# Three changes in a two-layer graph kernel: when layer 1's transfers go out, how many denominators are taken together, and which ready piece TensorE takes

## The chip, the cores and the metric

The kernel runs on one core of a Trainium2 chip. The core has TensorE (PE in the profile; matrix products, with PEld loading the weights), VectorE (DVE), ScalarE (ACT), GpSimd (POOL) and SyncE (SP), which here mostly issues the transfers. The metric is the time of one execution on the device in microseconds (us), lower being better.

## The reference, cut to what matters

Two layers of a graph network on 3327 nodes with 256 features. Layer 0 does two steps; in each, the features are multiplied by the row-normalised adjacency matrix (Xf) and by an attention matrix of which only the largest entries, 90% of each row's mass, are kept (Xa). Layer 1 is a graph attention with four heads of 64 features.

```python
h = relu(layernorm(x))
R = (adj + eye) / rowsum(adj + eye)
for n in range(2):                               # layer 0
    A  = top_p(softmax(q(Xa) @ k(Xa).T), 0.9)    # rows summed to 1 again
    Xf = R @ Xf
    Xa = A @ Xa
    Z  = Z + Xf @ U1[n].T + Xa @ U2[n].T
x = x + layernorm(h + Z)

hp = (relu(layernorm(x)) @ W).reshape(n, 4, 64)  # layer 1
e  = leaky_relu(s[:, :, None] + d[:, None, :])   # s, d: two numbers per node and head
e  = where(adj > 0, e, -inf)
x  = x + elu(softmax(e, axis=2) @ hp)
```

## The kernel before, in words

The nodes lie in 26 tiles of 128 (padded to 3328). All matrix products are in float32, so that the profile shows two TensorE records for one product.

**The planner.** The code doesn't issue instructions one after the other. It puts *pieces* of work into a `Plan` (L481, `put`), each with an engine, a length in us as its author estimates it, a rank (the due time, as it were: lower is earlier), the pieces that it needs, the buffers that it takes and gives back, and a lag until others see its result. `order` (L507) walks through an imagined time and, whenever an engine is free, takes among the pieces that are ready and whose buffers are free the one of lowest rank (L553). The pieces are then issued in the order that comes out, and each engine and each queue works through its own instructions strictly in that order, whatever the real times are.

**Layer 0.** For each of the two steps n and each row tile i there are two chains:

- *Attention* of row i. `search` (L1502): TensorE makes the logits, ScalarE their exponentials (tile e, or qq for every fifth row); ScalarE counts over the row for two or three guesses of the threshold with GpSimd's arithmetic between, then VectorE takes a window of candidates, sorts them, chooses the threshold and drops what lies below. `attention` (L1559): VectorE transposes 32 x 32 blocks, the three parts of the row go to DRAM (`put_blocks`, L1121) and come back turned (`get_blocks`, L1126, four transfers for each part), and TensorE multiplies them with the features in pieces of four, the last of six (`attend_blocks`, L1133, into the PSUM bank acca). All rows go by memory except the last row, 25, of the second step, which TensorE turns itself (L1090, L1108). Row 24 is thus the last turned row that travels through memory.
- *The adjacency row* t (`full`, L1594): SyncE loads 128 x 512 pieces of the transposed adjacency matrix (L1152) into six rotating tiles named at, and TensorE multiplies them in pieces of two (`some`, L1158) into the PSUM bank accf. There is one such bank. At the end of a row it is copied out by ScalarE or VectorE (L1169, L1172, L1175, L1179) before the next row can begin. In the second step GpSimd then adds a base that SyncE fetched (L1183, L1192).

After the second step each row is normalised (`finish2`, L1402) and projected with layer 1's weights (L1440, L1449); ScalarE's L1435 is the normalisation's last step before the transposes of L1440.

**Layer 1** (`attend_neighbours`, L1619). The result's columns are done in four blocks b of 832. Within a block, the loop j runs over the 26 tiles of source nodes. SyncE loads adjacency pieces (L1734; for j = 0 and 1 of the first block L1721, into the tile kt), ScalarE makes a mask of them (L1743 and L1744; L1728 and L1729), VectorE builds a tile of masked scores for the four heads (L1755, four instructions) from one of seven rotating tiles and from numbers broadcast over the partitions (`broadcast`, L1681, transfers L1688 into qq, for odd blocks into c). TensorE multiplies it with the features (products, L1771, into pl) and with the weights of the softmax's denominators (sums, L1785, into acca and accf). A tile of scores is given back when its sums are done. The sums of JG = 2 tiles are put together behind the products of those two; the last six j of the last block go one by one, in halves. When a block is done, ScalarE copies the banks out (L1843 to L1857), TensorE transposes (L1882), and the elu and the sum with x follow.

The transfers that open layer 1 have their own conditions: the first two adjacency pieces and the broadcast of block 0 need `open_heads` (all logits done, the counts of all rows done, the rows in qq done), the later adjacency pieces need all logits done.

Of the kernel before, what the change touches and what calls it, by code (L numbers as in the profile page):

```python
# [21 lines left out]
NT = 26  # L22
# [449 lines left out]
class Plan:  # L472
# [34 lines left out]
    def order(self):  # L507
# [17 lines left out]
        while len(out) < len(self.pieces):  # L525
            while events and events[0][0] <= clock:
                _, _, p, what = heapq.heappop(events)
                if what == "end":

                    held = sum(max(0.0, min(z, clock) - max(a, p["at"])) for a, z in holds[-12:])  # L530
                    end = p["at"] + p["length"] + held
                    if end > clock + 1e-6:
                        now[p["engine"]] = end
                        heapq.heappush(events, (end, p["k"], p, "end"))
                    else:
                        finish(p, clock)
                    continue
                if what not in ("", "own"):
                    free[what] += 1
                    continue  # L540
                for q in p["then"]:
                    if (q["engine"] == p["engine"]) == (what == "own"):
                        q["left"] -= 1
                        if not q["left"]:
                            for e in q["on"]:
                                ready[e].append(q)
            for e, queue in ready.items():
                if now[e] > clock or not queue:
                    continue
                can = [p for p in queue if all(free[b] >= p["take"].count(b) for b in p["take"])]  # L550
                if not can:
                    continue
                p = min(can, key=lambda q: q["rank"])  # L553
                for k in p["on"]:
                    ready[k].remove(p)
                p["engine"] = e
                p["length"], p["fn"], p["lag"], p["hold"] = p["on"][e]
                for b in p["take"]:
                    free[b] -= 1
                p["at"] = clock  # L560
                now[e] = clock + p["length"]
                if p["hold"]:
                    holds.append((clock, clock + p["hold"]))
                if e == "POOL":
                    heapq.heappush(events, (now[e], p["k"], p, "end"))
                else:
                    finish(p, now[e])
                out.append(p)
            if events and events[0][0] <= clock:
                continue  # L570
            times = [t for e, t in now.items() if t > clock and ready[e]] + ([events[0][0]] if events else [])
            later = [t for t in times if t > clock]
            if not later:
                if len(out) < len(self.pieces):
                    raise RuntimeError("the plan stands still")
                break
            clock = min(later)
# [10 lines left out]
def fast(  # L588
# [58 lines left out]
    with ExitStack() as l0:  # L647
# [911 lines left out]
        def attention(row, rank, total, drops, right):  # L1559
# [17 lines left out]
            for g in range(3):  # L1577
                b = plan.put(
                    "DVE", 1.17 if g < 2 else 1.44, rank - 1.001, row.turn_blocks, g, needs=[drops[g]]
                )  # L1580
                b = plan.put("SP", 0.5, rank - 1.0, row.put_blocks, g, needs=[b], lag=7.0)
                b = plan.put("", 0.0, -90.0, lambda: None, needs=[b], lag=0.0)
                come.append(
                    [plan.put("SP", 0.6, rank - 1.0, row.get_blocks, g, o, needs=[b], lag=5.0) for o in range(4)]
                )
            for j in range(0, NT - 2, 4):
                js = range(j, j + 4 if j < 20 else NT)
                a = plan.put(
                    "PE", 0.432 * len(js), rank, row.attend_blocks, js, needs=[come[j // 8], a, right],
                    take=["acca"] * (j == 0), give=[own_e[row.n][row.i]] * (j == 20),  # L1590
                )
            return plan.put("ACT", 0.4, rank - 2.7, row.attended, needs=[a, total], take=["xa"], give=["acca", "sc"])

        def full(n, t, rank, right, after):  # L1594
# [7 lines left out]
            for j in range(0, NT, 2):  # L1602
# [2 lines left out]
                    "PE", 0.437 * 2, rank, f.some, range(j, j + 2), needs=[a, loads[j // JC], right[j : j + 2], own if t in (j, j + 1) else None],  # L1605
                    take=["accf"] * (j == 0), give=["at"] * last,
                )
            if n == 1:
                a = plan.either(
                    ("ACT", 0.4, f.scaled_by_s), ("DVE", 0.45, f.scaled_by_v), -90.0, needs=[a], give=["accf"]  # L1610
# [8 lines left out]
        def attend_neighbours(rows, ends, done, fulls):  # L1619
# [1 line left out]

            W = NP // 4
            C = W // 2
            JG = 2
            LATE = 6
            logits_done = [r.pieces["logits"] for r in rows]
            freed = [p for p in done]
# [6 lines left out]
            def open_heads():  # L1634
                both = wpool.tile([P, NT, P], F32, name="qq").rearrange("p t d -> p (t d)")
                extra["both"] = [both.rearrange("p (h w) -> p h w", h=H)]

                extra["at"] = wpool.tile([P, 2 * W], F32, name="kt").rearrange("p (k w) -> p k w", k=2)
                extra["m"] = scr.tile([P, NP // 2], BF16, name="junk").rearrange("p (k w) -> p k w", k=2)

# [6 lines left out]
                extra["e"] += halves_of("rhs", None)  # L1647

            counted = [r.pieces["counted"] for r in rows]
            fifth = [d for d, name in zip(done, own_e[1]) if name == "e5"]  # L1650
            opened = [plan.put("", 0.0, 59.0, open_heads, needs=[logits_done, counted, fifth], lag=0.0)]
            opened.append(plan.put("", 0.0, 59.0, open_heads2, needs=[fulls, opened], lag=0.0))
            more = plan.put("", 0.0, 59.0, open_more, needs=[freed, opened], lag=0.0)

# [23 lines left out]
            cuts = (0, 7, 13, 20, NT)  # L1678
            spread = [spread_heads(*cuts[k : k + 2]) for k in range(4)]

            def broadcast(b, rank):  # L1681

                lo, hi = b * W, (b + 1) * W
                got, after = [], [spread[: b + 1], opened[b % 2], used_heads[b % 2]]
                for a in range(2):
# [4 lines left out]
                            highs[2 * a : 2 * a + 2, lo:hi].partition_broadcast(P),  # L1690
                        )

                    got.append(plan.put("SP", 0.1, rank, fetch, needs=[after], lag=7.0 + 5.0 * a))
                return got

            last, f_ = {}, None
            used_heads = [None, None]
            evacuated = [None, None]
            both = broadcast(0, 59.5)
            for b in range(4):  # L1700
                lo = b * W
                r0 = 60.0 + 10.0 * b
# [12 lines left out]
                for j in range(NT):  # L1715
# [77 lines left out]

                    own = ["mask"]
                    if b == 0 and j < 2:
                        loads = plan.put("SP", 0.2, rank, load_first, needs=[opened[0]], lag=4.0)
                        m_ = last_m = plan.put("ACT", 1.8, rank, mask_first, needs=[loads, last_m], take=own)
                    else:
                        loads = [
                            plan.put("SP", 0.4, rank, load, g, needs=[logits_done], take=["at"], lag=4.0)  # L1800
                            for g in range(2)
                        ]
                        m_ = last_m = plan.put("ACT", 2.2, rank, mask, needs=[loads, last_m], take=own, give=["at", "at"])
# [20 lines left out]
                        "PE", 1.42, max(rank, r0), product, 1, needs=[x_, y_, evacuated[1]], take=["pl"] * (j == 0)  # L1824
                    )
                    group.append((sums, mine))
                    if len(group) == JG or j == NT - 1 or (b == 3 and j == NT - LATE - 1):
                        for n_, (fn, name) in enumerate(group):
                            last_den = plan.put(
                                "PE", 1.52 - 0.06 * (n_ == 0), max(rank, r0), fn, needs=[last_acc, last_den, done if b == 0 else None],  # L1830
                                take=["acca", "accf"] * (j < JG and n_ == 0), give=[name],
                            )
                        group = []
                used_heads[b % 2] = last_e
# [298 lines left out]
```

## Time and profile before

| | us |
|---|---|
| median of 3 runs | 2049.98 |
| lowest and highest | 2047.79, 2050.27 |
| the profiled execution | 2050.93 |
| its span, first to last instruction | 2049.1 |
| TensorE busy | 2017.5 (98%) |
| VectorE busy | 1688.8 (82%) |
| ScalarE busy | 1298.0 (63%) |
| GpSimd busy | 1025.8 (50%) |
| DMA queue 1, share of 16 engines | 61.9% |

In time, the first 50 us prepare, layer 0's two steps run until about 1570 us, and layer 1 from there to the end. The profile names an instruction by its line in the kernel, its engine, and its output and inputs by the program's names. A wait is idle time of an engine just before an instruction, with the instruction that ended it; the chain is followed back from the last instruction to whatever released each step. The granted clock is TensorE's clock as a share of full speed.

### The profile page before, as it was taken

The numbers are of one execution on the slowest core, as the hardware profiler recorded it, in microseconds if no ns is written. First come the engines' busy times: TensorE is split into PE (matmuls) and PEld (weight loads), VectorE is DVE, ScalarE is ACT, GpSimd is POOL, SyncE is SP. The second block draws the span as 40 slices with busy tenths as digits, with TensorE's granted clock in tenths as the row PEclk, the third lists the DMA queues.
The fourth block names the chain that finished last, engine by engine and source line by source line (L and its number), as shares of the span: only waits on it lengthen the run. The fifth ranks groups of instructions, "written<-read, shape, count | busy, mean of one in ns | idle before, by whom it ended". The sixth has DMA issues, their size and how long they took to land. (4 is left out here: it accounts for less than half of the span.)

```text
span 2049.1 us, 33972 instructions
## 1 busy us (share of the span) xinstructions
PE 2017.5 (98%) x10526; PEld 1398.1 (68%) x10526; DVE 1688.8 (82%) x3763; ACT 1298.0 (63%) x2637; POOL 1025.8 (50%) x2222
## 2 busy tenths in 40 slices
PE   9999999999999999999999999999999999999997
PEld 6577778878777887788887877777876333333332
DVE  5589998987878845888788888888877999999894
ACT  5777777665667417866777777777634456475642
POOL 5377766765566615776777877778752000000001
PEclk9999999999999999999999999999999999999999
DMA  3276777867766776787577677676783354443440
GB/s 96 78 212 180 213 202 195 219 193 208 193 191 189 224 186 198 199 229 215 155 202 210 188 186 207 195 204 188 205 256 119 113 155 133 142 129 115 127 118 26
DMA packets 628991, 358.20 MB, mean 175 GB/s; under 512 B 366810, under 2 KB 581760, under 8 KB 628800
## 3 DMA queue, kind: packets, MB, share of 16 engines
q1 hardware_dynamic: 627904, 355.72, 61.9%
q8 instruction: 86, 1.41, 0.3%
q14 instruction: 105, 0.86, 0.1%
q10 hardware_dynamic: 896, 0.21, 0.0%
HBM read 252.69 MB, written 102.88 MB: 174 GB/s over the span
## 5 line engine op out<-in xcount | busy, mean ns | idle before, releaser
L1133 PE MATMUL acca<-rhs,e 128*128 128x256 f32 x2132 | 474.0, 381 | 4.4 <-DMA e<-blocks 4.4
L964 ACT ACTIVATE junk<-e,sc 128x3327 fp8e5<-128x3327 f32 x147 | 450.8, 3067 | 43.3 <-POOL sc L1001 41.8
L1133 PEld LDWEIGHTS acca<-rhs,e 128*128 128x128 f32 x2132 | 418.7, 197 | 52.3 <-DMA e<-blocks 4.8
L1158 PE MATMUL accf<-main,at 128*128 128x257 f32 x1352 | 316.6, 383 | 4.4 <-ACT f L1169 3.3
L1158 PE MATMUL accf<-c,at 128*128 128x256 f32 x1352 | 310.0, 382 | 6.4 <-DVE main L1175 4.2
L1158 PEld LDWEIGHTS accf<-main,at 128*128 128x128 f32 x1352 | 250.2, 190 | 63.2 <-issue 17.2
L1158 PEld LDWEIGHTS accf<-c,at 128*128 128x128 f32 x1352 | 252.1, 190 | 55.6 <-issue 9.9
L1027 DVE MAX8 cands<-y 128x8 f32<-128x205 f32 (+1 forms) x832 | 242.1, 361 | 3.6
L1744 ACT ACTIVATE junk<-at 128x448 bf16<-128x448 f32 (+1 forms) x204 | 112.2, 550 | 178.3 <-DVE e L1755 111.7
L1934 POOL TENSOR_TENSOR qq<-qq 128x256 f32<-128x256 f32 x4 | 2.9, 730 | 430.8 <-ACT qq L1930 430.7
L1022 DVE SCALAR_TENSOR_TENSOR y<-e,sc 128x1639 f32<-128x1639 f32 x84 | 165.7, 1972 | 48.4 <-POOL sc L1012 47.2
L1771 PE MATMUL pl<-e,main 128*64 128x416 f32 x1024 | 191.9, 517 | 0.0
L909 PE MATMUL pl<-kt,qg 64*128 64x512 f32 (+1 forms) x832 | 173.7, 536 | 1.4 <-ACT qq L926 0.8
L1078 DVE SCALAR_TENSOR_TENSOR e<-e,thr 128x1024 f32<-128x1024 f32 (+1 forms) x126 | 171.2, 1360 | 1.0
L1117 DVE STREAM_TRANSPOSE e<-e 128x1024 f32<-128x1024 f32 (+1 forms) x123 | 164.6, 1338 | 6.2
L926 ACT ACTIVATE e<-pl 128x1024 f32<-128x1024 f32 x123 | 134.9, 1105 | 53.0 <-PE pl L909 49.5
L1771 PEld LDWEIGHTS pl<-e,main 128*64 128x64 f32 x1024 | 69.5, 137 | 109.4 <-issue 91.8
L1755 DVE SCALAR_TENSOR_TENSOR e<-qq,low,junk 128x832 f32<-128x832 f32 x128 | 130.4, 1086 | 7.7 <-DMA qq<-highs 4.0
L1755 DVE SCALAR_TENSOR_TENSOR e<-c,low,junk 128x832 f32<-128x832 f32 x128 | 129.2, 1070 | 4.5 <-issue 3.2
L909 PEld LDWEIGHTS pl<-kt,qg 64*128 64x128 f32 x832 | 71.5, 186 | 85.9 <-issue 71.3
L964 ACT ACTIVATE junk<-qq,sc 128x3327 fp8e5<-128x3327 f32 x35 | 107.4, 3068 | 19.5 <-POOL sc L1001 19.2
L1133 PE MATMUL acca<-rhs,qq 128*128 128x256 f32 x520 | 114.7, 380 | 0.0
(553 smaller groups left out, 3366.6 us busy)
## 6 DMA issues: line engine op xcount, KB each, us to landing
at<-in_adjt_dram SPq DMA_DIRECT2D x414, 256.0 KB
blocks<-e SPq DMA_DIRECT2D x82, 512.0 KB
e<-blocks SPq DMA_DIRECT2D x328, 128.0 KB
blocks<-e SPq DMA_DIRECT2D x41, 640.0 KB
e<-blocks SPq DMA_DIRECT2D x164, 160.0 KB
at<-in_adjt_dram SPq DMA_DIRECT2D x102, 192.0 KB
blocks<-qq SPq DMA_DIRECT2D x20, 512.0 KB
qq<-blocks SPq DMA_DIRECT2D x80, 128.0 KB
```

Source lines behind the costliest of these rows:

```text
L909: T.matmul(pl[:, lo : lo + m], qg[self.n, self.i // 4][half, self.i % 4, :], kt[half, 512 * k : 512 * k + m], start=True, stop=True,)
L926: S.activation(to, pl.rearrange("p (g t q) -> p g t q", g=4, t=2), AF.Exp, accum_out=sums[k])
L964: S.activation(junk[:, :N], self.e[:, :N], fn, bias=t, scale=-1.0, accum_out=dst, saturate=False)
L1022: V.scalar_tensor_tensor(self.y[:, : hi - lo], self.e[:, lo:hi], self.up, self.e[:, lo:hi], ALU.is_lt, ALU.mult, accum_out=(self.h0, self. ...
L1027: V.max(self.cands[:, a * PIECES // 2 + k, :], self.y[:, at[k] - lo : at[k + 1] - lo])
L1078: V.scalar_tensor_tensor(piece, piece, self.thr[:, at : at + 1], piece, ALU.is_gt, ALU.mult)
L1117: V.transpose(part, part)
L1133: T.matmul(self.acc, lhs, rhs[self.n][:, j, :], start=(j == 0), stop=(j == NT - 1))
L1158: T.matmul(self.acc[:, : self.w], self.at[j // JC][:, j % JC, :], self.src[:, j, : self.w], start=(j == 0), stop=(j == NT - 1),)
L1744: S.activation(to, src, AF.Sign)
L1755: V.scalar_tensor_tensor(held["e"][:, k, :], extra["both"][b % 2][:, k, :], low[:, j, k : k + 1], held["mask"], ALU.max, ALU.mult,)
L1771: T.matmul(q["acc"][a][k * FH : (k + 1) * FH, c, :C], main[:, j, h * FH : (h + 1) * FH], held["e"][:, h, c * C : (c + 1) * C], start=(j == 0),
```

## The change

- *The pick of the planner.* Attention's pieces on TensorE by way of memory are marked `spare`, the later pieces of an adjacency row `fill` (j from 16 on, or from 20 on in the second step's rows from 14 on). If the ready piece of lowest rank is spare, and no spare piece waits only for it, then a fill piece is taken in its place if one is ready.
- *Layer 1's transfers.* `open_heads` is split: the broadcast tile needs only the rows that used it (rank 52), the tiles for the first adjacency pieces (`open_first`) still need logits and counts. The first half of block 0's broadcast is put behind the last read of row 23's blocks, the second half and all adjacency loads of layer 1 behind the last read of row 24's.
- *Denominators.* The sums are taken for four tiles at a time: in blocks 1 to 3, and in block 0 from j = 16 on (before that for two). The lengths given to the planner follow.

```diff
                 p = min(can, key=lambda q: q["rank"])
+                if p.get("spare") and not any(q.get("spare") and q["left"] == 1 for q in p["then"]):
+                    p = min((q for q in can if q.get("fill")), key=lambda q: q["rank"], default=p)
...
+            row.pieces["come"] = come
...
                     take=["acca"] * (j == 0), give=[own_e[row.n][row.i]] * (j == 20),
                 )
+                a["spare"] = True
...
                     take=["accf"] * (j == 0), give=["at"] * last,
                 )
+                a["fill"] = j >= (16 if n == 0 or t < 14 else 20)
...
-            JG = 2
...
+            def open_first():
                 extra["at"] = wpool.tile([P, 2 * W], F32, name="kt").rearrange("p (k w) -> p k w", k=2)
                 extra["m"] = scr.tile([P, NP // 2], BF16, name="junk").rearrange("p (k w) -> p k w", k=2)
...
+            turns = [r.pieces["come"][-1][-1] for r in rows if r.i < BLOCKED[1]]
+            came = turns[-1]
             fifth = [d for d, name in zip(done, own_e[1]) if name == "e5"]
-            opened = [plan.put("", 0.0, 59.0, open_heads, needs=[logits_done, counted, fifth], lag=0.0)]
+            opened = [plan.put("", 0.0, 52.0, open_heads, needs=[fifth], lag=0.0)]
+            room = plan.put("", 0.0, 59.0, open_first, needs=[logits_done, counted], lag=0.0)
...
-            def broadcast(b, rank):
+            def broadcast(b, rank, behind=()):
...
-                    got.append(plan.put("SP", 0.1, rank, fetch, needs=[after], lag=7.0 + 5.0 * a))
+                    got.append(plan.put("SP", 0.1, rank, fetch, needs=[after, behind[a : a + 1]], lag=7.0 + 5.0 * a))
...
-            both = broadcast(0, 59.5)
+            both = broadcast(0, 52.0, turns[-2:])
...
-                        loads = plan.put("SP", 0.2, rank, load_first, needs=[opened[0]], lag=4.0)
+                        loads = plan.put("SP", 0.2, rank, load_first, needs=[room, came], lag=4.0)
...
-                            plan.put("SP", 0.4, rank, load, g, needs=[logits_done], take=["at"], lag=4.0)
+                            plan.put("SP", 0.4, rank, load, g, needs=[logits_done, came], take=["at"], lag=4.0)
...
-                    if len(group) == JG or j == NT - 1 or (b == 3 and j == NT - LATE - 1):
+                    if len(group) == (4 if b or j > 15 else 2) or j == NT - 1 or (b == 3 and j == NT - LATE - 1):
                         for n_, (fn, name) in enumerate(group):
                             last_den = plan.put(
-                                "PE", 1.52 - 0.06 * (n_ == 0), max(rank, r0), fn, needs=[last_acc, last_den, done if b == 0 else None],
-                                take=["acca", "accf"] * (j < JG and n_ == 0), give=[name],
+                                "PE", 1.46 + 0.1 * (n_ == 0) + 0.1 * (n_ == len(group) - 1), max(rank, r0), fn, needs=[last_acc, last_den, done if b == 0 else None],
+                                take=["acca", "accf"] * (last_den is None), give=[name],
                             )
```

## The prediction

> **What bounds the kernel now.** First the page's busy times, then the chain of what ended last, then waits, then stretches of time around the place where the attention stage hands over to layer 1. The busy times (engine, busy us, share of the span, instructions):
>
> ```profile
> PE 2017.5 (98%) x10526; PEld 1398.1 (68%) x10526; DVE 1688.8 (82%) x3763; ACT 1298.0 (63%) x2637; POOL 1025.8 (50%) x2222
> ```
>
> TensorE (PE) is busy for all but 31.6 of 2049.1 us, and 15 of those lie in the first 51 and the last 50 us. So an edit gains by fewer TensorE microseconds, by idle gaps in between, or by the clock. The waits of TensorE, longest first (who waited, for whom: us, times, longest):
>
> ```profile
> PE acca L1133 <- DMA e<-blocks: 4.4, 4, 3.4
> PE accf L1158 <- DVE main L1175: 4.2, 8, 0.6
> PE accf L1158 <- ACT f L1169: 3.3, 6, 0.9
> ...
> PE accf L1158 <- ACT main L1172: 1.7, 3, 0.6
> PE accf L1158 <- DVE f L1179: 1.0, 2, 0.5
> ```
>
> Attention (L1133) waits once for long, 3.4 us; the adjacency rows (L1158) wait 20 times (with one for POOL, 0.5 us), 10.7 us, some 0.54 each: the single bank accf is being copied out while the next row wants it. The long wait, in TensorE's order of time (start, length, records, idle before):
>
> ```profile
> 1522.48 1.99 PE L1158 MATMUL accf<-c,at 128*128 128x256 f32 x8 [0.56 <-ACT main L1172]
> 1527.91 11.80 PE L1133 MATMUL acca<-rhs,e 128*128 128x256 f32 x40 [3.43 <-DMA e<-blocks]
> ```
>
> The same 40 records took 8.80 us for the row before. The windows say why (us, busy of each engine, granted clock, DMA share, GB/s):
>
> ```profile
> 1520.00:1530.00 10.00, 5.47 (x19) 3.88 (x18) 8.20 (x23) 0.47 (x1) 3.74 (x4) 0.85 1.02 290
> 1530.00:1540.00 10.00, 10.00 (x40) 8.60 (x40) 7.37 (x28) 0.63 (x2) 5.77 (x14) 0.81 0.67 184
> ```
>
> The granted clock fell to 0.85 and 0.81, so this stall costs 3.43 + (11.80 - 8.80) = 6.4 us. The SyncE queue just before it (start, time to issue):
>
> ```profile
> 1506.04 2.07 SPq L1721 DMA_DIRECT2D kt<-in_adjt_dram  x4
> 1508.16 0.94 SPq L1688 DMA_DIRECT2D qq<-highs  x2
> 1509.15 0.47 SPq L1121 DMA_DIRECT2D blocks<-e  x1
> ```
>
> Layer 1's first loads (2 x 416 KB of kt, 2 x 832 KB of qq: 2.5 MB) go out ahead of row 24's turned blocks, the last that travel by memory. Then layer 1, from the chain:
>
> ```profile
> 1828.80 5.74 PE pl L1771 x32
> 1834.54 0.84 PE acca L1785 x8
> 1837.47 5.74 PE pl L1771 x32
> ```
>
> A round of two j is 5.74 us of products and 2.93 of sums, without a gap.
>
> **The change part by part.** The sum is made against the profiled run, 2050.93 us (span 2049.1 and 1.8 around it), 0.95 above the median 2049.98 of the runs.
>
> *Denominators by four.* Arithmetic stays. In the chain, stretches of 8, 16 and 32 product records take 1.55, 2.94 and 5.74 us: 1.40 per 8 and 0.15 on entering. The first 8 sum records of a stretch take 0.83, later ones 0.70: 0.13. A round costs 0.28 us beyond its work. In the instruction order TensorE has 65 stretches of sums before and 45 after: 20 x 0.28 = **5.6 us less**. What could eat it is VectorE, which makes the four e tiles before their sums release them. One j costs it 3.985 us (back-to-back tiles start at 1829.19, 1833.17, 1837.15), TensorE 4.33. VectorE's idle time in the four blocks (1570-1690, 1690-1805, 1805-1920, 1920-2010) is 1.7, 4.7, 6.5 and 1.0 us, 13.9 against 5.6 wanted. Seven e tiles rotate, so j+7 is built in the tile of j. That comes free after four products and one sum (4 x 2.80 + 1.4 = 12.6 us into a group of 4 x 4.33 - 0.28 = 17.0), is filled by 16.6 and wanted at 17.0 + 3 x 2.80 = 25.4. So it holds. Bounds: 3 (VectorE paces the last block, and rounds beside transposes pay anyway) and 6.0 (20 x 0.30, the excess in the last rounds, 2.38 for 1.40 + 0.69).
>
> *Layer 1's loads behind row 24.* In the new SyncE order half of qq stands behind row 23's reads, the rest of qq and kt behind row 24's. Row 24's first put now stands behind two adjacency loads, which wait for a slot of the six at tiles that full row 24 (the adjacency product) frees at its j = 8-11. From that release TensorE has 32 matmuls x 0.4325 = 13.8 us, transposes 0.22, one projection 0.89 and one accf gap 0.56 until row 24's attention: 15.5 us, with 14 more adjacency matmuls ahead of it than before. The path against it: the load's issue 0.4, then put to first matmul, 16.5 us for row 23 (1480.12 to 1496.58, no DMA wait), 17.8 for row 22 (1451.25 to 1469.09, waited 0.18), 18.8 for row 24 with layer 1's bytes in flight (1509.15 to 1527.91). Without them I take the middle of the first two: 17.1 + 0.4 - 15.5 = 2.0 us still waited. Gain 6.4 - 2.0 = **4.4 us**. Bounds: 6.4 (no stall) and -0.3 (18.8 + 0.4 - 15.5 = 3.7, and the 3.0 of clock again).
>
> Does a 2.0 us wait lower the clock? In this trace waits up to 0.9 us left it at 1.00 and 3.43 did not; between them nothing is shown, so 0 to 3.0 us, and I take 0 for the nearer 0.9. The Trainium skill ("TensorE: Matmul & The Clock Gate", section "The HAM clock gate") has the clock halve only after an idle window of about 3.4 us and stay halved for about as long. By that rule the 2.0 us would cost themselves alone; the trace agrees at 3.43 us, where the excess was 3.0, and shows nothing between.
>
> The moved loads delay layer 1's first masks. ScalarE's queue has the first (L1728, on kt) ahead of a normalisation (L1435) whose transposes TensorE meets 20 matmuls into row 24's attention, about 1539. Put 2 goes out at about 1517.2, lands 9.7 us later (row 23's first put: 1480.12 to 1489.80), reads 2.4, qq 0.5, kt lands 4.4 after its issue (1506.04 to 1510.42): 1534.9, masks 1.8, normalisation 0.6: 1537.4. Cost 0, cover 1.7 us; the 832 KB of qq ahead, 2.9 us at 290 GB/s, would leave 1.2. VectorE, held by row 24's sum until about 1542, then builds j = 0, 1, 2 before TensorE's first sums at about 1566; before, j = 2 was begun at 1569.66. That costs nothing.
>
> *The last ready piece kept back.* Nothing is added; the planner's pick (L553) prefers late pieces of adjacency rows to the last ready attention piece. In TensorE's order 21 of 51 changes of accf had under 1 us of other work in between (the trace shows 20 waits), now 18: 3 x 0.54 = **1.6 us less**. Most others stay bare since attention pieces are all spent when the rows change, above all over the last nine. Everything behind a changed pick moves too: attention of rows 7 to 9 and 15 to 18 of the second pass starts 3 to 6 us of TensorE work earlier, and row 7's now took 15.96 us from put to first matmul (1019.35 to 1035.31), less than row 23's 16.5: no spare. Bounds: 10.7 (all waits covered) and -4 (short DMA waits at such rows; the nearest are 0.2 to 0.6 us each).
>
> Sum: 5.6 + 4.4 + 1.6 = 11.6; 2050.93 - 11.6 = 2039.3, against the median 2049.98 - 11.6 = **2038.4 us**.
>
> **The rivals.**
> 1. The stall returns through another queue: row 24's put behind the at loads costs what layer 1's loads cost. For it: SyncE waited for TensorE's at slots 16.2 us in 1440-1540. Against: 14 matmuls more cover. Gain 5.6 + 1.6 - 0.3 = 6.9: 2043.1.
> 2. The kept-back pieces cover all accf waits: 5.6 + 4.4 + 10.7 = 20.7: 2029.3. Against: 18 bare changes in the order.
> 3. VectorE paces layer 1 and the denominators bring nothing: 6.0 gained, 2044.0. For it: 89.04 of 90 us busy in the last block. Against: 13.9 us free in all.
> 4. Slower: attention that starts earlier in TensorE's order outruns its blocks. Place: the rows named above; price: each wait that reaches 3.43 us costs 6.4 with the clock. It needs three to beat 11.6 (19.2: 2057.6), with two it ends at 2051.2. Against: only four such waits before, three of them under 0.7 us.
>
> **How the numbers follow.** A measurement of this kernel can tell about 0.2% (4.1 us) from no change: 2045.9 to 2054.1 counts as the same. Forecast 0.50 (its own range 2034 to 2043), rival 1 0.20, rival 2 0.08, rival 3 0.08, rival 4 0.10, nothing moved 0.04. Faster: 0.50 + 0.08, most of rival 1 (0.15) and of rival 3 (0.05): 0.78. Same: 0.05 + 0.03 + 0.04 = 0.12. Slower: 0.10. The range leaves out rival 2 below, and rival 4 and the worse ends of 1 and 3 above: 2031 to 2046.
>
> **What would show it.** Denominators: 45 stretches of sums, those of four tiles 32 records long, products still 1.40 per 8, and no gap of TensorE before a product. Loads: row 24's attention with under 3 us of DMA wait and a granted clock of 1.00 in that stretch; first sums near 1566 instead of 1573.5. Kept piece: accf waits 9 us instead of 10.7. The prediction is wrong if a DMA wait over 3 us stands at any attention row, if the clock falls there, or if TensorE waits for e tiles in layer 1.

## The result, and the profile after

| | median, us | against before | ratio, 95% interval |
|---|---|---|---|
| before (in the same comparison) | 2050.26 | | |
| after | 2046.33 | -3.9 | 0.9980 [0.9973, 0.9988] |
| forecast | 2038.4 | -11.6 | |

A third of the forecast gain came, and the time lies just outside the range given. The profiled execution of after took 2042.61 us (span 2040.8), which is the fastest of its 12 runs (2042.61 to 2051.83); the pair of profiles therefore shows 8.3 us between the kernels where the medians show 3.9. Busy times of after, from its page:

```profile
PE 2008.4 (98%) x10526; PEld 1399.5 (69%) x10526; DVE 1690.6 (83%) x3772; ACT 1295.8 (63%) x2628; POOL 1040.0 (51%) x2222
```

TensorE is busy for 9.1 us less than before, and still idle for 32.4 us (31.6 before). So waits went and others came. The waits of TensorE in after (for whom: us, times, longest):

```profile
PE px L1442 <- ACT xa L1437: 5.2, 2, 2.9
PE accf L1160 <- DVE main L1177: 3.0, 6, 0.6
...
PE accf L1160 <- ACT f L1171: 1.9, 4, 0.5
...
PE acca L1135 <- DMA e<-blocks: 1.2, 2, 1.0
```

The long wait for row 24's blocks is gone (1.2 us in all, none of it at row 24), and the waits of the adjacency rows (L1160, accf) sum to 9.2 us instead of 10.7; four more of 1.7, 1.0, 1.0 and 0.6 us are left out above. On top now stands a wait that before did not have: two transposes (L1442) that wait for a normalisation on ScalarE (L1437; L1435 in before's lines). TensorE at the place, in after (start, length, records, idle before):

```profile
1514.85 0.44 PE L1442 MATMUL px<-ident,xa 128*128 128x128 f32 x2 [2.29 <-ACT xa L1437]
1515.12 1.71 PE L1160 MATMUL accf<-c,at 128*128 128x256 f32 x4
1516.62 1.97 PE L1451 MATMUL px<-late,xt 128*128 128x264 f32 x4
...
1528.89 8.80 PE L1135 MATMUL acca<-rhs,e 128*128 128x256 f32 x40
1540.62 0.44 PE L1442 MATMUL px<-ident,xa 128*128 128x128 f32 x2 [2.93 <-ACT xa L1437]
...
1543.49 1.05 PE L1451 MATMUL px<-late,xt 128*128 128x264 f32 x4
```

Row 24's attention (L1135 at 1528.89) runs without a wait and at full speed: 40 records in 8.80 us, not 11.80. But 2.29 us are lost ahead of it and 2.93 in the middle of it. After the first, the four records of L1451 take 1.97 us instead of the 1.05 that they take at 1543.49: the clock fell. One window of after (us, busy of each engine, granted clock, DMA share, GB/s):

```profile
1510.00:1520.00 10.00, 7.71 (x29) 6.16 (x28) 8.14 (x8) 4.99 (x19) 8.91 (x19) 0.83 0.81 262
```

The low clock has moved from 1520-1540, where it is now 1.00, to 1510-1520. Its excess there, against full-speed records of the same kind, is about 1.9 us. So 2.29 + 1.9 + 2.93 = 7.1 us stand where 6.4 stood before.

Who held ScalarE? First SyncE (time to issue), then ScalarE, both of after:

```profile
1529.66 0.72 SPq L1696 DMA_DIRECT2D qq<-highs  x1
1530.42 2.52 SPq L1729 DMA_DIRECT2D kt<-in_adjt_dram  x4
```

```profile
1538.24 0.90 ACT L1736 ACTIVATE kt<-kt 128x832 f32<-128x832 f32 x1 [17.28 <-DMA kt<-in_adjt_dram]
...
1539.98 0.59 ACT L1437 ACTIVATE xa<-ystage,mv 128x256 f32<-128x256 f32 x1
```

ScalarE stood idle for 17.28 us at layer 1's first mask, until kt had landed, 7.8 us after its issue (1530.42 to 1538.24); the normalisation L1437 is queued behind that mask, and it is what TensorE waits for at 1540.62. GpSimd had finished the number that it needs (mv, L700) at 1533.30, so the mask held it for 6.7 us. The other wait, at 1514.85, comes down another chain. GpSimd and VectorE in after:

```profile
1506.09 0.46 POOL L1167 TENSOR_TENSOR at<-at,ident 128x128 f32<-128x128 f32 x1 [7.90 <-DMA x1s<-ystage]
```

```profile
1509.11 0.49 DVE L1429 SCALAR_TENSOR_TENSOR ystage<-xa,mv,ystage 128x256 f32<-128x256 f32 x1 [5.46 <-POOL mv L698]
```

GpSimd waits for a transfer (the line names the store x1s; what the instruction reads is an adjacency tile, and move_qq_alone below names that load for the same wait), VectorE for GpSimd, ScalarE for them and TensorE for ScalarE. In SyncE's queue half of qq (832 KB) now goes out at 1496.40, just ahead of three adjacency loads (1497.29) and the store x1s (1499.32).

The denominators, in after's chain of what ended last (start, length, records):

```profile
1831.08 11.32 PE pl L1779 x64
...
1848.12 11.32 PE pl L1779 x64
```

Four tiles take 17.04 us from one product stretch to the next; before, two rounds of two took 2 x 8.67 = 17.34. That is 0.30 us per round saved, without a gap ahead of a product.

### The profile page after: what moved, and what is told of

It reads as the page before. It is cut to its first block, busy times and chain, and to the rows that moved or that the text cites. A ratio compares the mean times of both kernels' runs of the same rounds, so it can differ in the third digit from the quotient of the medians.

```text
span 2040.8 us, 34002 instructions
## 1 busy us (share of the span) xinstructions
PE 2008.4 (98%) x10526; PEld 1399.5 (69%) x10526; DVE 1690.6 (83%) x3772; ACT 1295.8 (63%) x2628; POOL 1040.0 (51%) x2222
## 4 chain that ended last, share of the span: by engine, by line
PE 94%; DMA 2%; POOL 1%; SPq 1%; ACT 1%; DVE 1%; issue 0%; DVEq 0%; POOLq 0%; ACTq 0%
PE accf L1160 28%; PE acca L1135 27%; PE pl L1779 15%; PE pl L911 8%; PE acca L1793 4%; PE accf L1793 4%; PE px L1354 2%; PE px L1451 1%; PE accf L1306 1%; PE acca L1306 1%; PE px L828 1%; PE px L1339 1%; PE acca L1110 1%; PE px L1890 1%; PE px L1254 1%; DMA at<-in_adjt_dram 1%
## 5 line engine op out<-in xcount | busy, mean ns | idle before, releaser
L1135 PE MATMUL acca<-rhs,e 128*128 128x256 f32 x2132 | 474.4, 380 | 2.8 <-ACT qd L1455 1.5
L1135 PEld LDWEIGHTS acca<-rhs,e 128*128 128x128 f32 x2132 | 416.6, 196 | 49.6 <-issue 2.3
L1160 PE MATMUL accf<-main,at 128*128 128x257 f32 x1352 | 316.4, 383 | 2.9 <-ACT f L1171 1.9
L1160 PE MATMUL accf<-c,at 128*128 128x256 f32 x1352 | 312.2, 383 | 6.3 <-DVE main L1177 3.0
L1160 PEld LDWEIGHTS accf<-c,at 128*128 128x128 f32 x1352 | 252.7, 190 | 55.4 <-issue 7.6
L1160 PEld LDWEIGHTS accf<-main,at 128*128 128x128 f32 x1352 | 250.3, 190 | 55.0 <-issue 11.7
L1763 DVE SCALAR_TENSOR_TENSOR e<-c,low,junk 128x832 f32<-128x832 f32 x128 | 129.0, 1071 | 11.5 <-issue 11.5
L1135 PE MATMUL acca<-rhs,qq 128*128 128x256 f32 x520 | 115.1, 379 | 0.0
L966 ACT ACTIVATE junk<-qq,sc 128x3327 fp8e5<-128x3327 f32 x35 | 107.5, 3070 | 11.5 <-POOL sc L1003 11.0
```

Source lines behind the costliest of these rows:

```text
L966: S.activation(junk[:, :N], self.e[:, :N], fn, bias=t, scale=-1.0, accum_out=dst, saturate=False)
L1135: T.matmul(self.acc, lhs, rhs[self.n][:, j, :], start=(j == 0), stop=(j == NT - 1))
L1160: T.matmul(self.acc[:, : self.w], self.at[j // JC][:, j % JC, :], self.src[:, j, : self.w], start=(j == 0), stop=(j == NT - 1),)
L1763: V.scalar_tensor_tensor(held["e"][:, k, :], extra["both"][b % 2][:, k, :], low[:, j, k : k + 1], held["mask"], ALU.max, ALU.mult,)
```

## The experiments

"Before" is measured in the same comparison each time: 2049.43 us for the first four, 2050.23 for the next four, 2050.98 for the last three. Differences are to that.

| run | what it is | median | difference | ratio, 95% interval |
|---|---|---|---|---|
| den_only | before + denominators by four | 2044.30 | -5.1 | 0.9975 [0.9966, 0.9984] |
| move_only | before + transfers moved | 2053.91 | +4.5 | 1.0025 [1.0016, 1.0034] |
| spare_only | before + kept-back piece | 2042.49 | -6.9 | 0.9967 [0.9955, 0.9979] |
| after_mask_later | after, masks told to come later | 2039.62 | -9.8 | 0.9948 [0.9935, 0.9962] |
| no_move | denominators + kept-back piece | 2038.70 | -11.5 | 0.9947 [0.9934, 0.9961] |
| move_mask_later | move_only, masks told to come later | 2055.27 | +5.0 | 1.0025 [1.0016, 1.0035] |
| kt_first | after, kt ahead of qq's second half | 2043.60 | -6.6 | 0.9971 [0.9960, 0.9982] |
| mask_later_qq_later | after_mask_later, all of qq behind row 24 | 2046.71 | -3.5 | 0.9983 [0.9974, 0.9992] |
| piece_not_late | no_move, kept-back piece not in the last rows | 2043.91 | -7.1 | 0.9963 [0.9950, 0.9977] |
| move_kt_alone | no_move + kt and at loads moved | 2041.25 | -9.7 | 0.9949 [0.9935, 0.9963] |
| move_qq_alone | no_move + broadcast moved | 2041.18 | -9.8 | 0.9950 [0.9937, 0.9964] |

The theory that these rows suggest: the denominators and the accf term are right, but the moved transfers cost waits that were put at nothing. The rival: attention that comes earlier in TensorE's order, a matter of the kept-back piece, causes the waits.

### The three parts, each alone

**den_only** takes the third part of the change alone:

```diff
-                    if len(group) == JG or j == NT - 1 or ...
+                    if len(group) == (4 if b or j > 15 else 2) or j == NT - 1 or ...
```

> The kernel before with the denominators by four and nothing else. Ledger theory (each part's price by the two traces): the stretch from the first to the last sums is 4.8 us shorter in the changed kernel, so 2050.3 - 4.8 = 2045.5 us, with 45 stretches of sums and the long DMA wait before row 24's attention (3.4 us and the slow clock behind it) as it was. Rival (VectorE paces layer 1, the gain was made elsewhere): 2048.5 or more, and VectorE busy over 99% in blocks 1 to 3.

Measured 2044.3: the term as worked out. The place is right too: from the first sums to the end of the span den_only takes 2042.9 - 1572.07 = 470.8 us, before 2049.1 - 1573.49 = 475.6, 4.8 less. The stall of row 24 is still there (2.90 us).

**move_only** takes the second part alone:

```diff
+            opened = [plan.put("", 0.0, 52.0, open_heads, needs=[fifth], lag=0.0)]
+            room = plan.put("", 0.0, 59.0, open_first, needs=[logits_done, counted], lag=0.0)
...
-            both = broadcast(0, 59.5)
+            both = broadcast(0, 52.0, turns[-2:])
...
+                        loads = plan.put("SP", 0.2, rank, load_first, needs=[room, came], lag=4.0)
```

> The kernel before with layer 1's transfers behind rows 23 and 24 and nothing else. Ledger theory: the DMA wait before row 24's attention goes (6.4 us with the clock), but ScalarE is held by the first mask until kt lands, and the half of qq behind row 23 delays the store and fetch that GpSimd waits for; the two give back nearly all: 2048 to 2051 us, with waits of the transposes L1440 on ScalarE's L1435 of 2 to 6 us in all. Rival (those two waits come from the new order of attention's pieces, not from the transfers): 2044 to 2046 us and no such wait.

Slower than both expectations, by 4.5 us against before. TensorE in move_only:

```profile
1523.46 7.15 PE L1133 MATMUL acca<-rhs,e 128*128 128x256 f32 x32 [0.81 <-DMA e<-blocks]
...
1539.71 1.84 PE L1449 MATMUL px<-late,xt 128*128 128x264 f32 x4 [4.55 <-ACT xt L1444]
...
1543.93 0.69 PE L1440 MATMUL px<-ident,xa 128*128 128x128 f32 x2 [2.39 <-ACT xa L1435]
```

The move does what it says: the stall of 3.43 us is down to 0.81. But 4.55 and 2.39 us follow, and the clock in 1540-1550 is 0.66. There is no kept-back piece in this kernel, so the rival (attention's order) falls.

**spare_only** takes the first part alone:

```diff
                 p = min(can, key=lambda q: q["rank"])
+                if p.get("spare") and not any(q.get("spare") and q["left"] == 1 for q in p["then"]):
+                    p = min((q for q in can if q.get("fill")), key=lambda q: q["rank"], default=p)
```

> The kernel before with the last ready attention piece kept back and nothing else. Ledger theory: 1.5 to 3 us faster by fewer accf waits (about 8.6 us in all instead of 10.7), long DMA wait at row 24 as before: 2047.3 to 2048.8 us. Rival (it only moves waits): within 1 us of before, or slower by a new wait.

Both missed: 6.9 us gained. The waits for accf fell as forecast (8.5 us). The rest is here, TensorE in spare_only:

```profile
1523.86 7.15 PE L1135 MATMUL acca<-rhs,e 128*128 128x256 f32 x32 [1.52 <-DMA e<-blocks]
```

Row 24's stall is down from 3.43 to 1.52 us, and the clock stays at 1.00 in every window from 1500 to 1570, with layer 1's transfers where they always were. TensorE does more adjacency work between row 23's attention and row 24's (34 matmuls, before 28), so it gets to row 24 later: 29.1 us after the start of row 23's attention instead of 27.9. The blocks come 0.7 us sooner by the same measure. The gain that the prediction booked to the transfers comes here without moving them.

The three alone sum to -5.1 + 4.5 - 6.9 = -7.5; together they give -3.9.

### What the transfers cost in the company of the other two

**no_move** is the change without its second part (the diffs of den_only and spare_only together).

> Denominators by four and the kept-back piece, with layer 1's transfers left where they were. The corrected theory (the kept-back piece alone covers row 24's stall by the 14 adjacency matmuls it puts ahead, and moving the transfers only costs) adds the two single runs: 2049.4 - 5.1 - 6.9 = 2037.4, so 2035.5 to 2039.5, with row 24's attention waiting under 2 us for its blocks at a granted clock of 1.00. The theory on record (the transfers' move is what takes the stall away) expects no more than the denominators' 5.1 and 2.2 of accf waits: 2042.1 or above.

2038.7, as the corrected theory adds up, and the lowest median of all the kernels run (the interval of after_mask_later, below, is the same but for 0.0001): 11.5 us under before and 7.6 under after (differences to before). TensorE in no_move:

```profile
1521.97 3.70 PE L1135 MATMUL acca<-rhs,e 128*128 128x256 f32 x16 [0.43 <-issue]
1525.97 3.70 PE L1135 MATMUL acca<-rhs,e 128*128 128x256 f32 x16 [0.30 <-DMA e<-blocks]
...
1539.59 1.06 PE L1092 MATMUL px<-ident,e 128*128 128x128 f32 x8 [1.04 <-DVE e L1080]
```

These three are TensorE's only waits of over 0.25 us between 1500 and 1570, 1.77 us in all where after has 5.78, and the clock is 1.00 throughout. The expectation's count is not right: by the traces 654 adjacency matmuls of the second step stand ahead of row 24's attention before, 662 in no_move, 658 in move_only and 668 in after. The 14 belong to the parts together, and the kept-back piece alone makes 8 of them. Between these two kernels the profiled spans differ by 4.4 us.

**piece_not_late** asks where the kept-back piece earns its 6.9 us:

```diff
-                a["fill"] = j >= (16 if n == 0 or t < 14 else 20)
+                a["fill"] = (n == 0 or t < 20) and j >= (16 if n == 0 or t < 14 else 20)
```

> no_move (denominators and kept-back piece, 2038.7 us) with the kept-back piece only up to adjacency row 19 of the second step: between row 23's attention and row 24's stand 28 adjacency matmuls again as before the change, instead of 34. If those few late matmuls are what covers row 24's stall, a wait of 2.5 to 3.5 us for its blocks and the clock below 1.00 behind it return: 4 to 7 us more, 2042.5 to 2045.5. If the kept-back piece gains by its other places (adjacency rows that wait less for their bank, over both steps), the time stays at 2037.5 to 2040.5.

2043.9, 4.5 us of the gain given back. TensorE in piece_not_late:

```profile
1523.61 10.36 PE L1135 MATMUL acca<-rhs,e 128*128 128x256 f32 x40 [3.51 <-DMA e<-blocks]
```

The stall and the slow clock are back: 3.51 - 0.73 of waiting and 10.36 - 8.80 of slow records are 4.3 us. So some 4.5 of the 6.9 us come from the last rows, where six adjacency matmuls more (34 instead of 28 between the two attentions, 6 x 0.43 = 2.6 us of work) stand ahead of row 24; the other 2.4 are the accf waits and what goes with them. The cover is not the whole of it. Counted from the start of row 23's attention, TensorE reaches row 24 at 27.2 us in piece_not_late and at 28.9 in no_move, 1.8 us later, while the blocks are there at 30.7 us in the one and by 29.4 in the other, at least 1.3 sooner. In no_move kt goes out 5.0 us ahead of row 24's first put, in piece_not_late and before 3.1; that its bytes are then less in the way is argued, and was not tried.

**move_kt_alone and move_qq_alone** split the move, on top of no_move (the second with `open_heads` split as in the change, which the diff below leaves out):

```diff
-                        loads = plan.put("SP", 0.2, rank, load_first, needs=[opened[0]], lag=4.0)
+                        loads = plan.put("SP", 0.2, rank, load_first, needs=[opened[0], came], lag=4.0)
...
-                            plan.put("SP", 0.4, rank, load, g, needs=[logits_done], take=["at"], lag=4.0)
+                            plan.put("SP", 0.4, rank, load, g, needs=[logits_done, came], take=["at"], lag=4.0)
```

```diff
...
-            both = broadcast(0, 59.5)
+            both = broadcast(0, 52.0, turns[-2:])
...
```

> no_move with only the adjacency loads of layer 1 (kt and those after it) put behind row 24's reads, the broadcast left ahead of row 24. If ScalarE held by the mask on kt is the larger part of what the move costs, TensorE waits 2 to 3 us for a normalisation behind that mask (kt lands about 4.4 us after its issue, with no broadcast ahead of it) and the clock may dip: 2040.5 to 2043.5. If the broadcast's place is the larger part: within 1 us of 2038.7.

> no_move with only the broadcast moved (one half behind row 23's reads, the other behind row 24's), kt and the other adjacency loads left ahead of row 24. If the half behind row 23 causes the 2.29 us wait and the clock of 0.83 behind it (by delaying an adjacency load and the store that GpSimd and VectorE stand behind), they show here too: 2041.5 to 2044.5. If kt is the larger part: within 1.5 us of 2038.7.

Each loses: against before they stand at -9.7 and -9.8, no_move at -11.5, so 1.8 and 1.7 us, while both together lose 7.6. The intervals of these two overlap with that of no_move, so the medians alone would not show it; the traces show a wait in each. TensorE in move_kt_alone, then in move_qq_alone:

```profile
1539.46 1.94 PE L1092 MATMUL px<-ident,e 128*128 128x128 f32 x8 [3.04 <-DVE e L1080]
```

```profile
1513.83 0.44 PE L1442 MATMUL px<-ident,xa 128*128 128x128 f32 x2 [0.92 <-ACT xa L1437]
...
1517.38 1.16 PE L1451 MATMUL px<-late,xt 128*128 128x264 f32 x4 [1.39 <-DVE xt L1446]
```

move_qq_alone has 2.3 us of waits where after has its 2.29 (GpSimd before it waits 7.36 us for an adjacency load), but the clock stays at 1.00. In move_kt_alone the planner put the normalisation's last step ahead of the mask (1525.02 against 1529.50), so the wait that was expected cannot show. The 3.04 us come down another chain: TensorE waits for VectorE, VectorE 3.37 us for GpSimd. SyncE and GpSimd in move_kt_alone:

```profile
1529.31 0.34 SPq L1414 DMA_DIRECT2D ystage<-in_x_dram  x1
```

```profile
1534.28 0.72 POOL L1417 TENSOR_TENSOR ystage<-ystage,late 128x256 f32<-128x256 f32 x1 [7.96 <-ACT sd L1460]
```

The line names a copy of ScalarE that stands behind the masks on kt, but that is only the last event before the start. GpSimd also waits for the load of ystage that the instruction reads. In no_move the same wait is put down to this load: L1417 starts at 1534.94, with GpSimd's own wait instruction (EVENT_SEMAPHORE) through at 1534.8. Here that one is through at 1534.1, when the load has landed. L1417 starts 0.16 us behind the landing in both kernels; so ScalarE's copy need not have held it at all. GpSimd starts 0.7 us sooner than in no_move, and TensorE gets its transposes at 1539.46, where no_move has 1539.59. What differs is that TensorE is there 2.1 us sooner, at 1536.42 instead of 1538.55. Layer 1's first products (8 records, 1.5 us), which no_move has ahead of row 24, stand later in the order since kt comes later, and 4 adjacency records less stand before the transposes. So here the later kt costs TensorE work to fill the time with, and the mask's hold is not the cause; behind the wait the clock falls to 0.93 and 0.73.

### Can the cost be planned away?

**after_mask_later and move_mask_later** tell the planner that kt lands after 9 us rather than 4, the one in after, the other in move_only:

```diff
-                        loads = plan.put("SP", 0.2, rank, load_first, needs=[room, came], lag=4.0)
+                        loads = plan.put("SP", 0.2, rank, load_first, needs=[room, came], lag=9.0)
```

> The changed kernel with one number altered: the planner is told that the first adjacency pieces of layer 1 land 9.0 us after their issue and not 4.0. In the instruction order the normalisation L1437 now stands ahead of the first mask L1736 on ScalarE and hardly anything else moves. Ledger theory: the 2.9 us wait of the transposes L1442 in row 24's attention goes and nothing takes its place, 2046.3 - 3 to 5 (some of its clock) = 2041.5 to 2043.5 us. Rival (TensorE is then held by the next thing, kt, qq or row 25's chain, for as long): 2045.5 to 2047 us.

> Only the transfers moved, as in move_only, and the planner told that the first adjacency pieces take 9 us to land instead of 4, so that ScalarE's normalisation steps stand ahead of the first mask. If move_only's loss of 4.5 us is ScalarE held by the mask on kt (waits of TensorE for xt and xa, 4.55 and 2.39 us, and the clock of 0.89 behind them), it goes: 2044 to 2048 (the stall of row 24 stays away, so up to 5 us under before). If the loss comes from the transfers themselves standing in the DMA queues at that time, it stays within 1.5 us of 2053.9.

In after it gains more than expected, 2039.62 (2036.87 to 2044.79). TensorE's instructions are the same ones in nearly the same order, and SyncE's order is that of after until 1564, so 5.9 of the 7.6 us that the move costs in after go when this one number is put nearer to the landing of kt. The gain of the move over no_move is still nothing. The profiled execution is the slowest of the five, so its waits don't say where the gain lies. They do show that the hold is not all gone; TensorE in after_mask_later:

```profile
1547.41 0.66 PE L1092 MATMUL px<-ident,e 128*128 128x128 f32 x4 [2.36 <-ACT sd L1460]
```

The 2.93 us for the normalisation are gone, and 2.36 us stand later, for copies of a projection (L1460) that are queued behind the mask; kt landed 8.7 us after its issue.

In move_only it gains nothing, 2055.27, and the expectation that ScalarE's hold is the loss falls there. GpSimd and TensorE in move_mask_later:

```profile
1539.30 1.44 POOL L1192 TENSOR_TENSOR main<-main,base 128x256 f32<-128x256 f32 x1 [9.45 <-DMA base<-ys]
```

```profile
1549.69 0.69 PE L1440 MATMUL px<-ident,xa 128*128 128x128 f32 x2 [5.66 <-ACT at L1101]
```

The masks no longer hold the normalisation, but GpSimd waits 9.45 us for base, a small load that SyncE issued only at 1534.59, behind kt and the adjacency loads. ScalarE then waits 7.47 us for GpSimd, makes the second mask, and only then copies a tile out (L1101) for which TensorE has waited 5.66. The first wait was cured and the second, behind it, came out.

**kt_first** puts the second half of the broadcast behind kt:

```diff
-                    got.append(plan.put("SP", 0.1, rank, fetch, needs=[after, behind[a : a + 1]], lag=7.0 + 5.0 * a))
+                    got.append(plan.put("SP", 0.1, rank + (2.5 * a if behind else 0.0), fetch, needs=[after, behind[a : a + 1]], lag=7.0 + 5.0 * a))
```

> The whole change, but the second half of the broadcast (832 KB of qq) issued behind kt's two pieces instead of ahead of them. If kt landed 7.8 us after its issue because of those bytes, it now lands about 3 us earlier (832 KB at 290 GB/s), ScalarE's wait for kt of 17.28 us ends as much earlier and TensorE's wait of 2.93 us for the normalisation behind it is under 0.5: 2042 to 2044.5. If kt's landing is set by something else (its own 128 x 832 pieces, the at loads), the wait keeps its 2.5 to 3 us and the time 2045.5 to 2047.

SyncE and ScalarE in kt_first:

```profile
1531.63 2.42 SPq L1729 DMA_DIRECT2D kt<-in_adjt_dram  x4
```

```profile
1536.02 0.90 ACT L1736 ACTIVATE kt<-kt 128x832 f32<-128x832 f32 x1 [16.03 <-DMA kt<-in_adjt_dram]
```

kt now lands 4.4 us after its issue, not 7.8: what stretched it were the 832 KB ahead of it. The time, 2043.6, is in the expected range, but not for the expected reason: TensorE's wait keeps 2.67 us, since the planner put the same transposes eight attention records (1.8 us) earlier. What else brought the 2.7 us against after, I can't name.

**mask_later_qq_later** puts both halves of the broadcast behind row 24:

```diff
-            both = broadcast(0, 52.0, turns[-2:])
+            both = broadcast(0, 52.0, [came, came])
```

> after_mask_later with the first half of the broadcast also behind row 24's reads, so that nothing of layer 1 is in the queues between row 23's and row 24's reads. If TensorE's wait of 2.29 us at 1514.85 and the clock of 0.83 behind it come from that half (it delays an adjacency load that GpSimd and then VectorE stand behind), about 2.3 + 1.9 = 4 us go: 2035 to 2038. If that wait is only the order of attention and adjacency rows, nothing changes or the later broadcast delays the first sums: 2039 to 2042.

Wrong by more than either: 2046.71. The 2.29 us wait and its low clock in 1510-1520 did go, but TensorE later has the longest wait of all these kernels:

```profile
1543.92 1.94 PE L1092 MATMUL px<-ident,e 128*128 128x128 f32 x8 [8.17 <-DVE e L1080]
```

SyncE, ScalarE and GpSimd in mask_later_qq_later, the last two lines from the view of L1417 (its wait instruction: length in ns, start) and from the timeline:

```profile
1524.87 7.34 SPq L1729 DMA_DIRECT2D kt<-in_adjt_dram  x4
...
1534.58 0.39 SPq L1414 DMA_DIRECT2D ystage<-in_x_dram  x1
```

```profile
1534.75 0.90 ACT L1736 ACTIVATE kt<-kt 128x832 f32<-128x832 f32 x1 [3.75 <-DMA kt<-in_adjt_dram]
```

```profile
L1417 POOLq EVENT_SEMAPHORE  x1: 43/43/43, 1538.6 to 1538.6; - x1
```

```profile
1538.75 0.72 POOL L1417 TENSOR_TENSOR ystage<-ystage,late 128x256 f32<-128x256 f32 x1 [14.01 <-ACT xa L1139]
```

Behind all of qq, kt lands 9.9 us after its first issue (1524.87 to 1534.75), and its four issues take 7.34 us instead of the 2.1 of no_move. The small load of ystage stands behind them and four adjacency loads in SyncE's queue: it goes out at 1534.58 and, by the semaphores in the trace, has landed at 1538.59, 4.0 us later, where no_move has 2.1 (1532.71 to 1534.78). GpSimd's wait instruction is through at once and L1417 starts 0.16 us after the landing, as in no_move. The line names row 24's copy-out on ScalarE (L1139, 1538.19 to 1538.65), which stands behind the masks and ended within 0.1 us of the landing; the load alone explains the start. VectorE has waited 9.74 us for GpSimd, TensorE 8.17 for VectorE. Of these 8.17 us, by the two timelines, 1.0 are in no_move too, 4.3 are the chain coming later and 2.8 are TensorE being there sooner, as in move_kt_alone.

## Why the prediction was wrong, point by point

- *What bounds the kernel*: right. Every difference is idle TensorE, slow records or fewer microseconds of TensorE.
- *Denominators by four, 5.6 us*: right; 5.1 alone, 0.30 per round against 0.28, no gap of TensorE ahead of a product. The condition that the seven tiles hold was met: VectorE has 112.7, 109.6, 109.6 and 86.5 us busy in the four stretches of 120, 115, 115 and 90, 418.4 in all where before has 426.2. Rival 3 falls.
- *Layer 1's loads behind row 24, 4.4 us gained*: this step failed, in two of its sentences. "14 more adjacency matmuls ahead of it than before" counts among the move's gains a cover of which the kept-back piece alone makes 8 matmuls, and with these the wait is small without the move (spare_only waits 1.52, no_move 0.73; piece_not_late takes them away in the last rows and has 3.51). By itself the move does shorten the wait, to 0.81 (move_only); beside the kept-back piece no more than 0.7 us was left for it to gain. The path was also mis-sized: from put to first matmul no_move takes 16.4 us with layer 1's bytes still ahead, where the step has 18.8 with them and 17.1 without. And "Cost 0, cover 1.7 us" was wrong: kt landed 7.8 us after its issue, not 4.4, so that the normalisation behind the first mask ended at 1540.57, where the step had 1537.4, and TensorE came to it at 1537.69, where the step had about 1539 (it named the 832 KB ahead of kt, and left them out of the sum). Its terms add up to 1534.2 for kt and 1536.6 for the normalisation, so the cover would have been 2.4 us; the landing, 3.4 us longer than taken, uses it up even so. The 4.4 us were read off the start of the first mask at 1510.42, where ScalarE was busy until then and did not wait for kt; kt_first shows the same 4.4 as a real landing, so the reading held by luck. Only that one instruction was costed, and not the others that ScalarE, GpSimd and SyncE have in the same stretch. The half of qq behind row 23 wasn't costed at all: with it GpSimd waits 7.4 us (move_qq_alone) to 7.9 us for a transfer, and TensorE 2.29 and 1.9 of clock. In all the move costs 7.6 us beside the other two parts, and 4.5 alone; 5.9 of the 7.6 go with the one number of after_mask_later.
- *The clock after a 2.0 us wait, taken at 0*: the 2.29 us wait lowered it, so the term is 1.9 in that place. That the trace of before agrees with a clock halved for about 3.4 us is too strong as well: 3.4 us at half the clock would lose 1.7 us, which is what piece_not_late shows (1.6 of excess behind 3.51 us), and not the 3.0 of before (behind 3.43).
- *Last ready piece kept back, 1.6 us*: the sum of accf waits came as forecast (9.2 in after, "9 instead of 10.7"). The part as a whole brought 6.9, because its effect on row 24 was booked elsewhere.
- *The sum*: 11.6 forecast, and 11.5 measured for the change without its second part. That the two agree is luck: a gain given to the wrong part, and a cost put at nothing, are two errors in the same step.
- *The rivals*: rival 1 (the stall returns through another queue) has the right form and the nearest time (2043.1 against 2046.3), but its queue is not row 24's put behind the at loads: it is ScalarE's, behind the mask that waits for kt (after, move_only), and SyncE's, where small loads (adjacency tiles, base, ystage) stand behind qq and kt. Rivals 2 and 4 don't appear.
- *What would show it*: row 24 under 3 us and at a clock of 1.00, yes; first sums near 1566, nearly (1568.37, where before has 1573.49); but first sums were a bad mark. no_move, faster by 7.6, has them at 1570.98, because the planner leaves other work of layer 0 for later. The sentence on what would make it wrong named a DMA wait at an attention row and VectorE in layer 1, not a wait for a normalisation, though the step itself gave it a cover of only 1.7 us.

## To carry to other kernels

When two parts of a change touch the same stall, work out the stall under each part alone before giving the gain to either: what is covered already can't be gained again. A bulk load that is moved is not finished with when its own consumer has time; list what is queued behind it on the issuing queue, and behind its first consumer on that engine, and price each by a landing with the bulk in flight. Where the cover of a "cost 0" is under two microseconds, run the change without that part first. And when a wait is put down to an engine, look at what else the instruction reads, and at the same wait in another run: a load may have landed at the same moment.

## What the runs showed of the hardware

- **When the clock falls.** Single waits of TensorE with the granted clock at 1.00 behind them: 1.52 us (spare_only), 2.13 (kt_first), 2.93 (after, at 1540.62). Waits with a lower clock behind them: 2.29 (after, 0.83), 2.67 (kt_first, 0.90 and 0.93 in the windows 1530-1540 and 1540-1550), 2.90 (den_only, 0.90 and 0.92), 3.04 (move_kt_alone, 0.73), 3.51 (piece_not_late, 0.83). Between about 2 and 3 us the length alone does not decide it. The Trainium skill ("TensorE: Matmul & The Clock Gate", section "The HAM clock gate") has an idle window of about 3.4 us; the waits of 2.29 to 3.04 us do not agree with it.
- **How much the clock takes.** The time lost by the clock, (1 - granted clock) x 10 us over the windows of a dip, has two sizes here: 1.7 or 1.8 us in after, den_only, kt_first and piece_not_late, and 3.4 or 3.5 in before, move_only, move_kt_alone, move_mask_later and mask_later_qq_later. The length of the wait doesn't choose between them either: 3.43 us in before stand with the larger, 3.51 in piece_not_late with the smaller.
- **Spread.** Runs of after lie between 2042.6 us (mean clock 0.998) and 2051.8 (0.995); those of no_move between 2038.2 and 2040.7. That after's two waits lie in the range in which the clock may or may not fall would explain the spread, and the 3.2 us by which the medians of these two differ more than their profiles; it was argued from these rows only, and not tried.
- **Landing behind bulk.** The same loads kt landed 4.4 us after their first issue with no broadcast just ahead of them (kt_first; 4.8 in move_kt_alone), 7.8 behind 832 KB of it (after; 8.7 in after_mask_later) and 9.9 behind 1664 KB (mask_later_qq_later): by the first figures 3.4 and 5.5 us more, where the 290 GB/s of before's window 1520-1530 would give 2.9 and 5.9. The 128 KB of ystage landed 2.1 us after their issue in no_move, 4.8 behind kt (move_kt_alone) and 4.0 behind qq and kt (mask_later_qq_later).
